# The last stage of a MoE-then-attention-convolution kernel, image by image in half-image slots

## The chip, the cores and the metric

One core of one Trainium2 chip runs the whole kernel. The metric is device microseconds of one launch. The kernel before takes 4912.13 us (median of 9 runs, 4890.7 to 4941.1). All data is 32-bit float in HBM at the start and at the end. The engines are TensorE (PE), VectorE (DVE), ScalarE (ACT), GpSimd (POOL) and SyncE (SP, used here to issue DMAs). Each has its own queue of instructions, works through it in order, and waits on semaphores of the others.

## What is computed

```python
# block 0: depthwise 7x7 conv, layer norm, mixture of 8 experts (2 per token), residual
x = depthwise_conv7x7(input) + dw_bias            # input: 32 x 128 x 56 x 56
x = layernorm_over_channels(x) * ln_gamma + ln_beta
moe = top2_of_8_experts_with_capacity(x)          # gelu MLP 128 -> 512 -> 128
h = input + x + layer_scale * moe
# block 1: coordinate attention, then a dense 3x3 convolution
y_h, y_w = h.mean(over w), h.mean(over h)         # pooled rows and columns
z = h_swish(bn1(w1 @ concat(y_h, y_w) + b1))      # 8 x (56 + 56)
a_h, a_w = sigmoid(wh @ z[:56] + bh), sigmoid(ww @ z[56:] + bw)
g = h * a_h * a_w                                 # the gated image
out = silu(bn2(conv3x3(g, wc) + bc))
...
```

## The kernel before

Four stages follow each other: the depthwise convolution (7x7, as matmuls with band matrices), the layer norm with the gates, the routing and the experts, and the last stage. The first three are the same in both kernels. They leave in HBM a table `acc_d` with one row of 137 numbers for each token in each of two parts: the row of a token's later expert (with the layer-normed x and that expert's share) and that of its earlier one. An image's sum is the two rows' first 128 numbers added.

The last stage works on pairs of images. There are 32 images, so 16 pairs; a pair has 6272 tokens, 49 tiles of 128.

- `load_pair` (L948) loads both images of x, 128 channels x 2 x 3136, in one DMA from SP.
- `combine` (L956 to L967), seven times a pair: two SP loads of 896 rows each (`cxn`, `cx2`; three buffers), POOL adds them (L959), PE transposes seven 128x128 tiles (L965), and DVE adds the transposed rows, beta and x into the image `x1` (L967). The first loads wait for a fence of DVE memsets (L855) behind the experts' last scatters.
- `squeeze` (L980 to L983): 1x1 matmuls of half an image into `pa`, then two DVE reductions (`rs`, `cs`).
- `attend`: the pooled sums (`rs` times weights L990, `ry` L991, PE L995 and L998), bn and h-swish on 8 partitions (`z`, L1001 to L1003), two matmuls (L1007, L1008), two sigmoids on ACT (L1009, L1010), then two gate products of 3136 elements on DVE (L1013 in place, L1014 into the padded image `pad`). Then POOL and ACT form, for the whole image at once, the six inputs `v` of a Winograd form F(4,3) along the rows: `t` (ACT L1021), `d` (POOL L1022), `twice` and `4d` (ACT L1024, L1025), `t` and the six sums (POOL L1026 to L1032).
- `conv` for half an image: six products k = 1, 2, 3, 4, 0, 5, three matmuls each (L1042; the profile counts each 32-bit matmul as two records), through five PSUM buffers. ACT copies product 1 (`odd`, L1047); DVE forms rows 0 and 1 of `y` from products 1 and 2 (L1048, L1049) and adds the other products in ten passes (L1052): four from product 3, four from 4, one each from 0 and 5. ACT applies silu (L1054) and issues the store (L1055).

The four halves' `conv` of a pair are spread over the seven `combine` steps of the next pair. The tile scheduler fixes each engine's order when the program is built, and adds the waits; inside an engine's queue nothing is overtaken at run time.

## Time and profile before

| what | value |
|---|---|
| median of 9 runs | 4912.13 us |
| profiled execution: run, span | 4901.19 us, 4899.2 us |
| busy in the span: PE, DVE, ACT, POOL | 3620.5 (74%), 2587.8 (53%), 1446.4 (30%), 2748.8 (56%) us |
| product matmuls L1042, 2304 records | 838.5 us |
| DVE passes L1052, 640 | 317.2 us, 552 ns each |
| POOL row adds L959, 112 | 269.6 us, 2415 ns each |
| POOL d L1022, 32 | 228.1 us, 7127 ns each |
| DVE gate products L1013, L1014, 32 each | 123.3 and 137.6 us |
| squeeze matmuls L980, 512 records | 146.0 us |
| transposes L965, 784 | 108.6 us |

Rows of a timeline give the start (us), the duration, engine, line and operation, output and inputs with their shapes, and in brackets the idle time before with what ended it. Matmuls overlap in the pipeline, so a row's duration is longer than the distance to the next start. A row with "x4" is a group of four that follow each other.

### The profile page before, as it was taken

To read this page: it belongs to the slowest core of one execution; us is meant where nothing else is said; L and a number is where in the kernel's file an instruction comes from. 1 tells how busy PE (TensorE), PEld (TensorE's weight loads), DVE (VectorE), ACT (ScalarE), POOL (GpSimd) and SP (SyncE) were. 2 spreads that over 40 slices of the span, in tenths; PEclk is the share of its full clock that TensorE was granted. 3 is DMA by queue.
4 is the path that set the end of the run, shared out by engine and by line. 5 is a ranking of instruction groups with operands and counts; after the bars stand their busy time and mean duration, and the time that the engine had idled before them with its cause. 6 is when DMAs were issued, how large, how long until landed. Compare 5 with 4: busy or idle time off the path is not lost. (4 is left out here: it accounts for less than half of the span.)

```text
span 4899.2 us, 60979 instructions
## 1 busy us (share of the span) xinstructions
PE 3620.5 (74%) x21765; PEld 2029.4 (41%) x21765; DVE 2587.8 (53%) x5562; ACT 1446.4 (30%) x3123; POOL 2748.8 (56%) x2044
## 2 busy tenths in 40 slices
PE   7999888841576486576457756677775999999999
PEld 4455588831233243233223323233332454444444
DVE  3333369996365267474411211111125888888887
ACT  0000066630233232233223323233341333332323
POOL 5444333421556654465555455555556978788875
PEclk9999997765688787788778877778887999999999
DMA  9999956549511211111111111111115555555552
GB/s 174 181 191 189 164 216 244 242 163 337 182 38 34 51 36 36 35 39 41 44 40 38 43 43 41 44 39 39 40 42 171 174 190 192 162 194 184 188 166 78
DMA packets 678004, 580.90 MB, mean 119 GB/s; under 512 B 405849, under 2 KB 611185, under 8 KB 667249
## 3 DMA queue, kind: packets, MB, share of 16 engines
q1 hardware_dynamic: 411408, 319.81, 22.7%
q10 hardware_dynamic: 222816, 160.70, 12.5%
q0 software_dynamic: 43264, 94.64, 7.2%
q8 instruction: 186, 3.05, 0.3%
q14 instruction: 330, 2.70, 0.2%
HBM read 314.92 MB, written 260.09 MB: 117 GB/s over the span
## 5 line engine op out<-in xcount | busy, mean ns | idle before, releaser
L703 POOL DMA_INDIRECT acc_d<-yo,row x676 | 700.6, 1036 | 760.3 <-issue 467.9
L662 PE MATMUL ph<-fxt,w 128*128 128x512 f32 (+1 forms) x1400 | 755.1, 677 | 378.2 <-ACT ht L663 346.7
L1042 PE MATMUL pc<-v,wk 128*128 128x392 f32 x1920 | 701.7, 508 | 0.4 <-POOL v L1027 0.4
L663 ACT ACTIVATE ht<-ph,bias 128x512 f32<-128x512 f32 (+1 forms) x700 | 473.4, 682 | 702.1 <-remote 306.6
L670 PE MATMUL py<-ht,w 128*128 128x512 f32 (+1 forms) x1400 | 653.7, 611 | 0.0
L641 POOL DMA_INDIRECT xg_r<-acc_d,idx x556 | 542.0, 975 | 198.7 <-issue 157.6
L165 PE MATMUL acc<-xs,band 28*64 28x432 f32 (+1 forms) x11264 | 535.6, 527 | 60.1 <-issue 37.8
L662 PEld LDWEIGHTS ph<-fxt,w 128*128 128x128 f32 x1400 | 279.1, 216 | 702.0 <-ACT ht L663 424.7
L1042 PEld LDWEIGHTS pc<-v,wk 128*128 128x128 f32 x1920 | 346.6, 190 | 306.8 <-issue 102.1
L165 PEld LDWEIGHTS acc<-xs,band 28*64 28x64 f32 x11264 | 299.0, 132 | 296.1 <-issue 199.0
L310 PE MATMUL lnps<-proj,lnyt 128*128 128x136 f32 x1568 | 364.8, 402 | 67.9 <-ACT sq L315 38.8
L670 PEld LDWEIGHTS py<-ht,w 128*128 128x128 f32 x1400 | 269.2, 201 | 284.9 <-issue 283.0
L310 PEld LDWEIGHTS lnps<-proj,lnyt 128*128 128x128 f32 x1568 | 351.0, 317 | 82.2 <-ACT sq L315 47.8
L654 DVE COPY fxt<-pt 128x512 f32<-128x512 f32 (+1 forms) x175 | 119.3, 682 | 445.7 <-remote 215.1
L697 DVE TENSOR_TENSOR ys<-pb,xg_r 128x512 f32<-128x512 f32 (+2 forms) x147 | 98.3, 671 | 450.0 <-PE pb L679 200.4
L1052 DVE SCALAR_TENSOR_TENSOR y<-pc,y 128x392 f32<-128x392 f32 x640 | 317.2, 552 | 11.7 <-PE pc L1042 11.7
L672 ACT ACTIVATE fyt<-py,b 128x512 f32<-128x512 f32 (+1 forms) x175 | 119.4, 682 | 674.9 <-PE py L670 472.2
L959 POOL TENSOR_TENSOR cxn<-cxn,cx 128x896 f32<-128x896 f32 x112 | 269.6, 2415 | 74.4 <-DMA cxn<-acc_d 25.8
L1022 POOL TENSOR_TENSOR d<-pad 128x3248 f32<-128x3248 f32 x32 | 228.1, 7127 | 143.6 <-DVE pad L1014 143.6
L448 PE MATMUL ps_r<-cnt_r,ones 128*128 128x1 f32 x400 | 84.1, 291 | 291.8 <-DVE junk L447 181.0
L181 DVE TENSOR_TENSOR yt<-acc,m 128x448 f32<-128x448 f32 x256 | 146.2, 619 | 264.4 <-PE acc L165 174.1
L641 POOL DMA_INDIRECT xg_f<-acc_d,idx x120 | 115.4, 962 | 224.4 <-DVE thr_r L460 90.0
(244 smaller groups left out, 5259.7 us busy)
## 6 DMA issues: line engine op xcount, KB each, us to landing
acc_d<-xn SPq DMA_DIRECT2D x16, 3356.5 KB
acc_d<-yo ACTq DMA_DIRECT2D x4, 13426.0 KB
lnyt<-y_d SPq DMA_DIRECT2D x16, 3136.0 KB
x<-in_x SPq DMA_DIRECT2D x16, 3136.0 KB
cxn<-acc_d SPq DMA_DIRECT2D x112, 448.0 KB
cx<-acc_d SPq DMA_DIRECT2D x112, 448.0 KB
out<-y ACTq DMA_DIRECT2D x64, 784.0 KB
xt<-in_x SPq DMA_DIRECT2D x64, 392.0 KB
```

Of the source, the lines that this page charges most:

```text
L165: nc.tensor.matmul(acc[r][half * M : (half + 1) * M, :, lo:hi], lhsT=band[rows, t0 + o - least, 1 - par : 1 - par + M], rhs=xs[i][rows, ha ...
L181: nc.vector.tensor_tensor(yts[r][:, :, i - 1 : W : 2], acc[r], common[r], ALU.add)
L310: nc.tensor.matmul(ps[:, j, :], lhsT=yf[:, self.j0 + g + j, :], rhs=proj, start=True, stop=True)
L641: d = nc.gpsimd.indirect_dma_start(out=xg[0:n, k, :], out_offset=None, in_=acc_d[0:T1, :], in_offset=bass.IndirectOffsetOnAxis(ap=idx[0][0 ...
L662: nc.tensor.matmul(ph[:, 0:N_], lhsT=w[0][:, f * P : (f + 1) * P], rhs=xt[:, 0:N_], start=True, stop=True)
L663: nc.scalar.activation(ht[:, f, 0:N_], ph[:, 0:N_], AF.Gelu, bias=w[2][:, f : f + 1])
L670: nc.tensor.matmul(py[:, 0:N_], lhsT=w2[:, f, :], rhs=ht[:, f, 0:N_], start=(f == 0), stop=(f == NF - 1))
L703: d = nc.gpsimd.indirect_dma_start(out=acc_d[:, :], out_offset=bass.IndirectOffsetOnAxis(ap=row[0:n, k : k + 1], axis=0), in_=yo[0:n, k, : ...
L959: nc.gpsimd.tensor_tensor(xn, xn, x2, ALU.add)
L1022: nc.gpsimd.tensor_tensor(d, high, low, ALU.subtract)
L1042: nc.tensor.matmul(m[k], lhsT=wk[k][:, dw, :], rhs=v[:, k, rows, dw : dw + W], start=(dw == 0), stop=(dw == 2))
L1052: nc.vector.scalar_tensor_tensor(r[x], m[k], f, r[y_], ALU.mult, ALU.add)
```

## The change

Only the last stage is rewritten. It goes image by image; image k has a slot, and the slot's list interleaves work on image k with products of image k-1 (upper half, `ch` 0) and k-2 (lower half, `ch` 1).

- x and the two parts of rows are loaded in blocks of eight image rows (448 tokens): one DMA of x and two of acc_d, 224 KB each, seven blocks an image, six buffers of each kind. The loads of block m+6 follow block m. Tables have 112 partitions x 4 tokens.
- The row adds of blocks with an even number (0, 2, 4, 6) run on POOL, of 1, 3, 5 on DVE. `merge` transposes four 112-token tiles and writes the eight rows at once into the padded image; the gate products then work in place there.
- `d`, `t` and `v` are formed for half an image at a time, in two parts; there is one buffer of `d` and of `t`, one `v` and one `y` for each half, and one `odd`.
- The small loads go to ACT's queue, the pads' borders alone are cleared (on DVE), and the stage's tiles wait for their own memory and not for the whole pool.

```diff
+    cp1 = ctx.enter_context(tc.tile_pool(name="cc", bufs=1, reuse_waits="tile"))
+    psp = ctx.enter_context(tc.tile_pool(name="cps", bufs=1, space=PSUM))
+    trp = ctx.enter_context(tc.tile_pool(name="ctr", bufs=2, space=PSUM))
+    pcp = ctx.enter_context(tc.tile_pool(name="cpc", bufs=5, space=PSUM))
+    MB = 8
+    NM = H // MB
+    MT = 2 * W
+    NX = 6
...
-            nc.sync.dma_start(t, a[name])
+        nc.scalar.dma_start(t, a[name])
...
+    def load_x(m):
+        nc.sync.dma_start(xss[m % NX], a["x"][m // NM][:, m % NM * MB : (m % NM + 1) * MB, :])
+    def load_rows(m):
+        for i, t in enumerate(cxs[m % NX]):
+            r0 = i * T1 + m * MB * W
+            d = nc.sync.dma_start(t, acc_d[r0 : r0 + MB * W, 0:C].rearrange("(j p) c -> p j c", p=MT))
+            for x in fence:
+                after(d.ins, x)
+    for m in range(NX):
+        load_x(m)
+    for m in range(NX):
+        load_rows(m)
...
-            nc.gpsimd.memset(t, 0.0)
+        nc.vector.memset(t[:, 0 : H + 2 : H + 1, :], 0.0)
+        nc.vector.memset(t[:, :, 0 : W + 2 : W + 1], 0.0)
...
+    def summed(m):
+        if m < NM * N:
+            x, x2 = cxs[m % NX]
+            (nc.vector if m % NM % 2 else nc.gpsimd).tensor_tensor(x, x, x2, ALU.add)
+    def merge(k, q):
+        m = NM * k + q
+        pt = trp.tile([P, BLK * P], F32, tag="tr", name=f"cpt{k}_{q}")[:, 0 : BLK * MT]
+        for j in range(BLK):
+            nc.tensor.transpose(pt[:, j * MT : (j + 1) * MT], cxs[m % NX][0][:, j, :], ident[0:MT, 0:MT])
+        nc.vector.scalar_tensor_tensor(pads[k % 2][:, 1 + q * MB : 1 + (q + 1) * MB, 1 : W + 1],
+                                       pt.rearrange("c (r w) -> c r w", w=W), beta_c, xss[m % NX], ALU.add, ALU.add)
+        if m + NX < NM * N:
+            load_x(m + NX)
+            load_rows(m + NX)
+        summed(m + 3)
...
+    def gate(n):
+        img = pads[n % 2][:, 1 : H + 1, 1 : W + 1]
+        nc.vector.tensor_tensor(img, img, bc(aw.unsqueeze(1), [C, H, W]), ALU.mult)
+        nc.vector.tensor_tensor(img, img, bc(ah.unsqueeze(2), [C, H, W]), ALU.mult)
+    def combined(n, ch, part):
+        v, pad = vs[ch], pads[n % 2]
+        r0 = 4 * RP * ch
+        byq = lambda x: x.rearrange("c (g r) w -> c g r w", r=4)
+        low, high = byq(pad[:, r0 : r0 + 4 * RP, :]), byq(pad[:, r0 + 2 : r0 + 2 + 4 * RP, :])
+        d, t = d_t, t_t
+        if part == 0:
             nc.scalar.mul(t, low[:, :, 1:3, :], 4.0)
             nc.gpsimd.tensor_tensor(d, high, low, ALU.subtract)
             nc.gpsimd.tensor_tensor(t, high[:, :, 1:3, :], t, ALU.subtract)
             nc.gpsimd.tensor_tensor(v[:, 1], t[:, :, 1, :], t[:, :, 0, :], ALU.add)
             nc.gpsimd.tensor_tensor(v[:, 2], t[:, :, 1, :], t[:, :, 0, :], ALU.subtract)
+        else:
+            nc.scalar.mul(v[:, 3], d[:, :, 1, :], 2.0)
+            nc.scalar.mul(d[:, :, 0:2, :], d[:, :, 0:2, :], 4.0)
+            nc.gpsimd.tensor_tensor(v[:, 4], d[:, :, 2, :], v[:, 3], ALU.subtract)
+            nc.gpsimd.tensor_tensor(v[:, 3], d[:, :, 2, :], v[:, 3], ALU.add)
             nc.gpsimd.tensor_tensor(v[:, 0], d[:, :, 2, :], d[:, :, 0, :], ALU.subtract)
             nc.gpsimd.tensor_tensor(v[:, 5], d[:, :, 3, :], d[:, :, 1, :], ALU.subtract)
...
+    def conv(n, ch, ks):
+        y = ys[ch]
+        r = [y[:, :, k, :] for k in range(4)]
+        m = {k: product(n, ch, k) for k in ks}
+        if 1 in m:
             nc.scalar.copy(odd, m[1])
             nc.vector.tensor_tensor(r[0], m[2], odd, ALU.add)
             nc.vector.tensor_tensor(r[1], odd, m[2], ALU.subtract)
...
+    def slots(k):
+        new = lambda f, *x: (lambda: f(*x)) if k < N else None
+        old = lambda d, f, *x: (lambda: f(k - d, *x)) if 0 <= k - d < N else None
+        cv = lambda *ks: old(2, conv, 1, ks)
+        pieces = [new(merge, k, 0), cv(1, 2), old(1, combined, 0, 1), new(merge, k, 1), new(merge, k, 2), cv(3),
+                  new(merge, k, 3), new(squeeze, k, 0), cv(4), new(merge, k, 4), new(merge, k, 5), cv(0), new(merge, k, 6),
+                  new(squeeze, k, 1), cv(5)]
+        cv = lambda *ks: old(1, conv, 0, ks)
+        pieces += [old(1, combined, 1, 0), new(pooled, k), cv(1, 2), new(attend, k), old(1, combined, 1, 1), cv(3),
+                   new(gate, k), cv(4), cv(0), cv(5), new(combined, k, 0, 0)]
+        return [f for f in pieces if f]
+    for m in range(3):
+        summed(m)
+    for k in range(N + 2):
+        for f in slots(k):
+            f()
```

In the new file the row add is L972, the transposes L978, the merge L979, the squeezes L990, their reductions L992 and L993, the weighting L998, `ry` L999, the pooled matmuls L1002 and L1005, `z` L1006 to L1008, the attention matmuls L1012 and L1013, the sigmoids L1014 and L1015, the gate products L1019 and L1020, `t` L1030 (ACT) and L1032 (POOL), `d` L1031, the v sums L1033 to L1041, `2d` and `4d` L1036 and L1037, the products L1049, `odd` L1058, rows 0 and 1 of y L1059 and L1060, the passes L1063, silu and store L1066 and L1067.

The scheduler again interleaves the lists by its own estimates. The order that the built program gives the engines in the slot of image k, once all stages of the pipeline are filled, is this ("(k,3)" is block 3 of image k, "product (k-1,0) 1" is product 1 of the upper half of image k-1, d0 and d1 are the d of upper and lower half):

```
POOL: row add (k,6) | d0 of k-1, t0, row add (k+1,0), v1, v2, v4, v3, row add (k+1,2), v0, v5 |
      t1, d1, v1, v2, v4, row add (k+1,4), v3, v0, v5 | row add (k+1,6)
ACT:  t0 of k-1, silu (k-2,0), 2d0, store, 4d0, t1, 2d1, 4d1, odd (k-1,0), silu (k-2,1), store,
      table load, two sigmoids of k, odd (k-1,1)
DVE:  merge (k,0), rows 0 1 of (k-2,1), merges (k,1) (k,2), 4 passes, merge (k,3), 1 pass, rs cs, 3 passes,
      merges (k,4) (k,5), row add (k+1,1), 1 pass, merge (k,6), 1 pass, row add (k+1,3), rs cs, weighting,
      row 0 of (k-1,0), ry, row 1, row add (k+1,5), z (with 2 passes between), 2 passes, 4 passes,
      gate product of k, 1 pass, gate product of k, 1 pass
PE:   products (k-2,1) 1 2 3 4 0 5 with merges' transposes and squeezes between,
      products (k-1,0) 1 2 and two of the three matmuls of 3, pooled matmuls (wait for ry),
      the rest of 3, product 4, attention matmuls (wait for z), products 0 5
```

In the slot of image 1, where nothing of k-2 exists, POOL's order is d0, t0, v4, v1, v2, v3, v0, v5, two row adds, d1; ACT has 2d1, odd (0,0) and 4d1 ahead of the two sigmoids of image 1; `ry` stands ahead of row 0 on DVE.

On SP, the second table load of block (k+1,5) waits for POOL's row add (k,6), and what follows it in the queue waits with it.

More of the change, by code (lines that the diff above doesn't have):

```diff
@@ new lines, in moe_conv_then_coordatt_kernel @@
+    xss = [cp1.tile([C, MB, W], F32, name=f"xs{k}") for k in range(NX)]
+    cxs = [[cp1.tile([MT, BLK, C], F32, name=f"cx{i}_{k}") for i in range(2)] for k in range(NX)]
+    def load_x(m):
[6 more added lines that the diff above has]
+                after(d.ins, x)
@@ new lines, in moe_conv_then_coordatt_kernel @@
+    for k in range(1, 5):
+        nc.vector.tensor_scalar(wk[k], wk[k], 1.0 / 6.0 if k > 2 else -1.0 / 6.0, None, ALU.mult)
+    nc.vector.tensor_scalar(wk[0], w0, 0.25, None, ALU.mult)
+    w1t = cp1.tile([C, QP], F32, name="w1t")
+    nc.vector.memset(w1t, 0.0)
+    nc.scalar.dma_start(w1t[:, 0:MIP], a["w1"])
+    quarter = [x / 56 for x in (7.0, 3.0, 1.0, 1.0)]
+    wq = cp1.tile([P, 4], F32, name="wq")
+    for k in range(4):
+        nc.vector.memset(wq[:, k : k + 1], quarter[k])
+    pick = [ident[:, QP * j : QP * j + MIP] for j in range(4)]
@@ new lines, in squeeze @@
+    def squeeze(n, half):
+        pad = pads[n % 2]
+        for j in range(4):
+            r0 = 1 + (4 * half + j) * SR
+            nc.tensor.matmul(pa[j * QP : (j + 1) * QP, 0 : SR * W], lhsT=w1t, rhs=pad[:, r0 : r0 + SR, 1 : W + 1],
+                             start=True, stop=True)
+        nc.vector.tensor_reduce(rs[:, half], pa[:, 0 : SR * W].rearrange("p (r q v) -> p r q v", r=SR, q=4), AX.X, ALU.add)
+        nc.vector.tensor_reduce(cs[:, half, :], pa[:, 0 : SR * W].rearrange("p (r w) -> p w r", r=SR), AX.X, ALU.add)
```

274 lines of the change are left out of this document (90 added, 184 removed).

## The prediction

> **What bounds the kernel now.** I read the page's slices first, then the stretches of the last stage, then its chain of waits, then the timeline of one pair of images, engine by engine. All times are of the one profiled execution (span 4899.2 us, run 4901.19 us; the median of the runs is 4912.13 us, 11 us more). The last stage, the only one that the change touches, begins when TensorE (PE) stops at 3699.8 us and lasts to the end: 1199 us. Two of its stretches:
>
> ```profile
> 3700.00:3720.00 20.00, 0.00 (x0) 0.00 (x0) 11.24 (x43) 0.00 (x0) 12.29 (x16) 0.57 0.36 122
> ...
> 4100.00:4250.00 150.00, 142.01 (x547) 74.81 (x546) 129.24 (x174) 45.59 (x45) 114.24 (x48) 1.00 0.58 185
> ```
>
> The numbers are busy us of PE, weight loads, VectorE (DVE), ScalarE (ACT), GpSimd (POOL), then the granted clock and the DMA share. In steady state PE is busy 95%, DVE 86%, POOL 76%; at the start PE has nothing. The chain of waits gives the beat, the same place in two successive pairs:
>
> ```profile
> 4064.11 6.12 PE pc L1042 x18
> ...
> 4134.62 6.12 PE pc L1042 x18
> ```
>
> 70.5 us for two images, 35.25 us each. PE's timeline holds where it waits:
>
> ```profile
> 4127.14 2.24 PE L1042 MATMUL pc<-v,wk 128*128 128x392 f32 x6
> 4130.41 0.36 PE L995 MATMUL cpa<-ry,ident 128*8 128x14 f32 x8 [1.03 <-DVE ry L991]
> ...
> 4133.97 0.42 PE L1007 MATMUL cpa<-z,wht 8*128 8x56 f32 x2 [0.82 <-DVE z L1003]
> ```
>
> Two waits for DVE, about 2.1 us an image. So an image is 33.15 us of PE work and 2.1 us of waiting: PE bounds the steady state. DVE's and POOL's timelines show what stretches DVE:
>
> ```profile
> 4100.41 3.41 DVE L1013 TENSOR_TENSOR x<-x,aw 128x3136 f32<-128x3136 f32 x1
> 4103.74 0.55 DVE L1052 SCALAR_TENSOR_TENSOR y<-pc,y 128x392 f32<-128x392 f32 x1
> ...
> 4128.20 1.91 DVE L990 TENSOR_TENSOR rs<-rs,wq 128x56 f32<-128x56 f32 x1
> ```
> ```profile
> 4109.19 7.16 POOL L1022 TENSOR_TENSOR d<-pad 128x3248 f32<-128x3248 f32 x1 [3.43 <-DVE pad L1014]
> 4116.26 3.11 POOL L1026 TENSOR_TENSOR t<-pad,t 128x1624 f32<-128x1624 f32 x1
> 4119.29 2.11 POOL L959 TENSOR_TENSOR cxn<-cxn,cx 128x896 f32<-128x896 f32 x1
> 4121.34 1.64 POOL L1027 TENSOR_TENSOR v<-t 128x812 f32<-128x812 f32 x1
> ...
> 4127.97 2.07 POOL L959 TENSOR_TENSOR cxn<-cxn,cx 128x896 f32<-128x896 f32 x1
> ```
>
> The 56-element L990 took 0.35 us at 3742.23, where POOL was idle; here it ends at 4130.11, just after POOL's row add (4130.04). A DVE instruction with both inputs in SBUF waits out the POOL instruction that runs. The reverse holds: at 3770.40 a v sum of POOL took 4.94 us instead of 1.76, behind a gate product of DVE. ACT's timeline, for the copy that starts a product's DVE passes:
>
> ```profile
> 4116.39 0.88 ACT L1024 ACTIVATE twice<-d 128x812 f32<-128x812 f32 x1 [2.29 <-POOL d L1022]
> 4117.30 1.56 ACT L1025 ACTIVATE d<-d 128x1624 f32<-128x1624 f32 x1
> ...
> 4126.47 0.48 ACT L1047 COPY odd<-pc 128x392 f32<-128x392 f32 x1 [2.40 <-PE pc L1042]
> ```
>
> Now ACT does d's multiples soon after d, one block for the whole image, and then idles until the product.
>
> **The change, part by part.**
>
> **PE work: no change.** Same 36 product matmuls (0.66 us each, from 18 records in 5.93 us) and eight squeezes an image; 28 transposes of 112 columns for 24.5 of 128: the same 3136 columns. Ten product runs instead of eight add two switches of 0.19 us (2 records take 0.85, their share of a long run 0.66); the squeezes pair up a little better. 33.2 us an image.
>
> **DVE: +1.8 us of work.** Three row adds an image (96 of 224): 512 elements at the gate product's 3.41/3136 = 1.09 ns are 0.6 us, each with a wait behind POOL. POOL's instructions are halved, so a wait is 0 to 1.2 us where the unhalved ones cost 1.0 to 2.0.
>
> **POOL: about 2.4 us less work** (four row adds of 1.2 us, 2.05 x 512/896, for 3.5 of 2.05; the rest halved and doubled in number). Nothing from that alone: POOL was not the bound.
>
> **Half images and the order.** Here I expect the loss. In the built program ACT's queue holds, in every slot: 2d and 4d of the second half, then the copy "odd" of product (k-1,0), then the rest. So the copy waits for the second d on POOL, which stands behind the whole first half. DVE's r0 (L1059) waits for the copy, and the reduction ry stands behind r0 in DVE's queue; PE's pooled matmuls (L1002) wait for ry, z follows, then the sigmoids and the two gate products, and the next image's first d waits for these. That is a closed loop over four engines, once per image. From the end of one second gate product to the next:
>
> - POOL: row add 1.2, d 3.55, t 1.5, add 1.2, v1 and v2 1.6, v4 and v3 1.75, add 1.2, v0 and v5 1.9, t 1.5, d 3.55 = 18.95 us (halves of the start-to-start times 7.1, 3.0, 1.6, 1.75, 1.9). Halving isn't exact: 812 elements start 1.59 us apart, 1624 need 3.01, which leaves 0.17 fixed, so ten halves cost 0.85 more: 19.8.
> - POOL held up by DVE's adds: two of 0.6 fall here, 0 to 1.2; I take 0.6.
> - ACT: 0.45 + 0.8 + 0.5 = 1.75 (halves of 0.88 and 1.56, the copy).
> - DVE: r0 0.5, ry 0.2; then r1 0.5, row add 0.6 with a wait of 0 to 1.2 (I take 1.0, a row add of POOL being next to it), z 0.35, a pass 0.5, r 0.2, a pass 0.5, z 0.15 with a wait of 0 to 1.2 (0.6: mean of the ends), six passes 2.85, gate 3.4, pass 0.45, gate 3.4 = 15.2. The sigmoids (1.2 us from L1012) hide under the six passes.
> - six hand-overs of 0.05: 0.3.
>
> Sum 19.8 + 0.6 + 1.75 + 15.2 + 0.3 = 37.65; I take **37.6 us** a slot. Bounds: all uncertain waits at nothing and POOL's first row add done before the gate (it needs rows asked for only after the transposes of (k,0), some 5 us before the gate ends) give 33.4, below PE's own 33.2 + 1.8 = 35.0, so 35; all at their tops 39.1, and late row loads 40. PE then idles 4.4 us a slot.
>
> On such idling the trace says: after 5.08 us of waiting (3847.20) the clock was 0.50 and twelve product records took 6.53 us instead of 4.22; after 2.53 us (3885.64) it stayed whole. [...] By the rows a drop costs 2.3 us of PE, which has 4.4 to spare: the sum stays too.
>
> **Loads.** 21 DMAs of 224 KB an image on SP's one queue instead of 7.5 larger ones. SP's issue takes 0.36 us: 7.6 of 37 us. Bytes are the same, DMA share stays near 0.56. Rows arrive at 346 GB/s (3726 to 3730 us), so one load moves in 0.7 us; the tightest has 6 us (rows (k+1,5), asked for after the transposes of (k,6), read by DVE's third add). Cost nothing; the cover gone, it is rival 3.
> [...]
>
> **Start.** Rows can leave at 3709.7, when the fence's memsets end, instead of 3714.35 behind fifteen small loads, and no longer share with a 3.1 MB image (7 us at 445 GB/s). DVE's constants, 3709.7 to 3721.6 before, lose POOL's pad memset beside them (3.6 us) and waits on loads: to 3717. Then three adds, seven merges, four reductions and their turns with PE, 10 us; z and sigmoids 6; gates with adds between 8: image 0 gated at 3741 (before 3755.4). Image 1: POOL's first-slot order 17.0, ACT 2.4, gates 7.25: 3768 (before 3786.4). Gain 18 us, uncertain by 8.
>
> **End.** After the last gate product: 2 products (4.1) and three halves at 11.86 us (4872.84 to 4884.70) less the 9.4 us run since the sigmoid matmul, 30.3, and the tail after the last product pass begins, 6.7: 37 to 38 (before 51.6, four halves). Gain 13.6.
>
> Sum: 3768 + 30 x 37.6 + 38 = 4934, against 4899.2: +35 us. Before: 3786.4 + 30 x 35.37 + 51.6. The two ends give 32 us back, 30 slots lose 67. Even at 36.4 us a slot.
>
> **Rivals.**
> 1. *PE still bounds (faster).* If POOL reaches the second d 2.6 us earlier (row add before the gate, adds that don't meet), the loop falls to 35: 3768 + 1050 + 38 = 4856, -43 us. For it: POOL has only 26 us of work; against: the loop's order is fixed in the queues and PE has no part in it. It decides from 36.4 us a slot downwards.
> 2. *Even.* Slots of 35.9 to 36.9 us: the ends' gains pay for the loop. Time within 15 us.
> 3. *Loads late.* SP's queue is in order, and a load behind a wait on POOL's last add holds up the others; if rows take over 6 us, DVE's third add stalls in the loop: 39.5 us, 4991, +92. Against: DMA share 0.58, and waits on row loads were 18 us in 840.
>
> **How the numbers follow.** Forecast (37 to 39 us a slot) 0.55, rival 1 0.22, rival 2 0.15, rival 3 0.08. On the median: 4912 + 35 = 4947, said as 4946. The likeliest case alone spans 4929 to 4989; with rival 1 the range is 4872 to 4990. Faster by over 0.3% (15 us, about what a measurement here tells from no change) 0.22, same 0.15, slower 0.63.
>
> **What would show it.** A beat of 37 to 38 us between gate products; PE's longest wait, 2 to 4 us, before L1002 for ry; before it r0 waiting for "odd", the copy for 4d, that for POOL's second d; POOL's d waiting for the gate. Wrong if L1002's wait is under 1 us, if the beat is 35, or if row adds wait on DMA.

## The result, and the profile after

The changed kernel takes 5071.95 us, median of 14 runs (5061.28 to 5088.6). The kernel before takes 4911.97 us, median of 46 (4882.72 to 4941.1). The ratio is 1.0329, with an interval of 1.0313 to 1.0346: slower by 160 us, where 35 were forecast. The direction was right; the time lies above the range. The profiled execution has a span of 5059.2 us.

The stretches come first (window, its length, busy us of PE, weight loads, VectorE (DVE), ScalarE (ACT) and GpSimd (POOL), granted clock, DMA share, GB/s):

```profile
3700.00:3720.00 20.00, 2.27 (x9) 1.51 (x10) 9.45 (x56) 0.00 (x0) 7.74 (x11) 0.55 0.51 131
4150.00:4300.00 150.00, 123.81 (x470) 64.45 (x468) 135.92 (x156) 42.40 (x49) 106.83 (x73) 0.92 0.56 157
```

PE was busy 95% of its steady state and is now busy 83%. DVE is the busiest engine, 91%, though it was given little work; the DMA share is about what it was (0.56 for 0.58).

The last stage begins when PE ends its last expert matmul, here at 3699.2 us. It took 1199.4 us before and takes 1360.0: this is the whole loss. Three pieces make it up. The time from its start to the second image's second gate product was 86.7 us and is 82.8. The mean beat between gate products was 35.37 us and is 41.24. The time from the last gate product to the end was 51.6 us and is 40.0. Both ends gained, 15.5 us together; thirty slots lost 5.87 us each.

The chain of waits of one slot (start, us, what; between the same place in two successive slots):

```profile
4059.56 4.15 PE pc L1049 x12
...
4080.13 1.18 DVE pad L979 x2
4081.31 1.28 DVE cx L972
4082.60 7.70 issue
4090.30 0.55 DVE y L1063
4090.85 0.60 DVE pad L979
4091.45 0.04 issue
4091.50 1.52 PE pa L990 x4
...
4100.55 4.15 PE pc L1049 x12
```

41.0 us for a slot. Up to 4078 the chain is PE's own work; then it goes through DVE: two merges, one of the new row adds (L972), 7.70 us in which the chain names no releaser, the merge of block 6, and only then the second half's squeeze. DVE's timeline shows what the 7.70 us are, and POOL's what went on meanwhile:

```profile
4080.05 1.26 DVE L979 SCALAR_TENSOR_TENSOR pad<-cpt,beta_c,xs 128x448 f32<-128x448 f32 x2
4081.23 9.14 DVE L972 TENSOR_TENSOR cx<-cx,cx 112x512 f32<-112x512 f32 x1
...
4091.84 2.06 DVE L972 TENSOR_TENSOR cx<-cx,cx 112x512 f32<-112x512 f32 x1
...
4096.49 0.68 DVE L972 TENSOR_TENSOR cx<-cx,cx 112x512 f32<-112x512 f32 x1
```
```profile
4080.89 1.06 POOL L1040 TENSOR_TENSOR v<-d_t 128x406 f32<-128x406 f32 x1
4081.89 1.07 POOL L1041 TENSOR_TENSOR v<-d_t 128x406 f32<-128x406 f32 x1
4082.91 1.64 POOL L1032 TENSOR_TENSOR t_t<-pad,t_t 128x812 f32<-128x812 f32 x1
4084.49 3.62 POOL L1031 TENSOR_TENSOR d_t<-pad 128x1624 f32<-128x1624 f32 x1
4088.05 0.91 POOL L1033 TENSOR_TENSOR v<-t_t 128x406 f32<-128x406 f32 x1
4088.91 0.92 POOL L1034 TENSOR_TENSOR v<-t_t 128x406 f32<-128x406 f32 x1
4089.78 1.42 POOL L1038 TENSOR_TENSOR v<-d_t,v 128x406 f32<-128x406 f32 x1
```

The same add takes 0.68 us when it meets nothing (4096.49). The one at 4081.23 found L1040 running, and POOL then started L1041, L1032, L1031, L1033 and L1034 ahead of it. It got in at about 4089.7 (its end less 0.68 us), where L1038 is the longer for it (1.42 us; the same sum took 0.97 at 4077.63). So it did not wait only for the instruction that was running; it lost five changes from one POOL instruction to the next. A "lost change" is counted so from here on: a POOL instruction that started while a DVE instruction with inputs in SBUF was held up. I counted them from the records of the last stage: of the 96 adds on DVE 38 lost none, 6 one, 26 two, 1 three, 17 five and 8 six.

The page's groups of the row adds (count, busy us and mean ns, then idle time before them):

```profile
L972 POOL TENSOR_TENSOR cx<-cx,cx 112x512 f32<-112x512 f32 x128 | 204.6, 1599 | 401.1 <-DMA cx<-acc_d 203.1
...
L972 DVE TENSOR_TENSOR cx<-cx,cx 112x512 f32<-112x512 f32 x96 | 378.5, 3943 | 4.4 <-DMA cx<-acc_d 4.3
```

3.94 us against 0.68: 3.26 us of being held up on the mean, three times an image. Most of it falls on the first of the three, which stands ahead of block 6's merge: its records are 7.9 us long on the mean (9.0 to 10.3 in nearly all late slots), the second's 2.8 and the third's 1.1. PE pays at the squeeze behind it, as its longest waits say (us in total, times, longest; over 1000 us from 3900):

```profile
PE pa L990 <- DVE pad L979: 165.0, 24, 7.8
```

6.9 us an image. Behind such a wait PE is slow as well: from 4091.5 to 4093.0 the granted clock is 0.50, as it is over the first 1.5 us behind each of the 26 waits of 5.0 to 7.9 us from 3925 on. Its timeline has groups of the same sizes at a clock of 1.00 before (4078 to 4083) and after it (4097 to 4100):

```profile
4082.45 0.85 PE L990 MATMUL pa<-pad,w1t 128*32 128x392 f32 x4
...
4091.50 1.52 PE L990 MATMUL pa<-pad,w1t 128*32 128x392 f32 x4 [6.68 <-DVE pad L979]
4092.95 3.70 PE L1049 MATMUL pc<-v,wk 128*128 128x392 f32 x8
...
4097.07 2.90 PE L1049 MATMUL pc<-v,wk 128*128 128x392 f32 x8
```

1.5 us more in this slot. The wait and the slow work are about the 8.0 us between 41.24 and PE's own 33.2.

### The profile page after: what moved, and what is told of

Its sections match the earlier page's. It is cut to its first block, busy times and chain, and to the rows that moved or that the text cites. A ratio compares the mean times of both kernels' runs of the same rounds, so it can differ in the third digit from the quotient of the medians.

```text
span 5059.2 us, 62785 instructions
## 1 busy us (share of the span) xinstructions
PE 3685.3 (73%) x21877; PEld 2035.1 (40%) x21877; DVE 2815.9 (56%) x5668; ACT 1463.0 (29%) x3219; POOL 2733.6 (54%) x2309
## 5 line engine op out<-in xcount | busy, mean ns | idle before, releaser
L1049 PE MATMUL pc<-v,wk 128*128 128x392 f32 x2304 | 871.7, 521 | 0.0
L165 PE MATMUL acc<-xs,band 28*64 28x432 f32 (+2 forms) x11264 | 555.8, 541 | 54.8 <-DVE yt L181 25.5
L1049 PEld LDWEIGHTS pc<-v,wk 128*128 128x128 f32 x2304 | 432.2, 199 | 357.4 <-issue 129.9
L972 POOL TENSOR_TENSOR cx<-cx,cx 112x512 f32<-112x512 f32 x128 | 204.6, 1599 | 401.1 <-DMA cx<-acc_d 203.1
L165 PEld LDWEIGHTS acc<-xs,band 28*64 28x64 f32 x11264 | 286.7, 136 | 323.4 <-issue 228.5
L972 DVE TENSOR_TENSOR cx<-cx,cx 112x512 f32<-112x512 f32 x96 | 378.5, 3943 | 4.4 <-DMA cx<-acc_d 4.3
L1063 DVE SCALAR_TENSOR_TENSOR y<-pc,y 128x392 f32<-128x392 f32 x640 | 327.3, 551 | 27.1 <-PE pc L1049 26.1
L990 PE MATMUL pa<-pad,w1t 128*32 128x392 f32 x512 | 160.5, 589 | 189.4 <-DVE pad L979 189.4
```

The lines of the kernel that those rows point to most:

```text
L165: nc.tensor.matmul(acc[r][half * M : (half + 1) * M, :, lo:hi], lhsT=band[rows, t0 + o - least, 1 - par : 1 - par + M], rhs=xs[i][rows, ha ...
L972: (nc.vector if m % NM % 2 else nc.gpsimd).tensor_tensor(x, x, x2, ALU.add)
L990: nc.tensor.matmul(pa[j * QP : (j + 1) * QP, 0 : SR * W], lhsT=w1t, rhs=pad[:, r0 : r0 + SR, 1 : W + 1], start=True, stop=True)
L1049: nc.tensor.matmul(m, lhsT=wk[k][:, dw, :], rhs=vs[ch][:, k, :, dw : dw + W], start=(dw == 0), stop=(dw == 2))
L1063: nc.vector.scalar_tensor_tensor(r[x], m[k], f, r[y_], ALU.mult, ALU.add)
```

## The experiments

The theories were these. The forecast's ring of four engines is right and only its term for the adds' waits is too small; then adds that aren't held up give about 37.6 us a slot (theory A in the expectations). Or the adds as work are too much for either engine; then the place they go to decides. Or the ring is tied by ACT's order ("odd" behind 4d); then moving that copy decides (G). Or PE bounds once DVE is free. Later came one on the shape: that a tile of 112 partitions is what makes DVE lose (D), against one by which POOL keeps DVE out whenever its own next instruction is ready (E). How a shape would do that, no run shows; "the port" in the expectations is the author's name for whatever lets one of the two engines in at a time, and no run shows it either.

A diff is against the changed kernel unless another is named. The table has the ratio to the kernel before on the same chip, and three numbers of the one profiled execution: the last stage, the mean beat, and from the stage's start to the second image's second gate product. Some chips ran the stages ahead of the last one some 580 us faster (in e1 it began at 3122.7 us, in the kernel before at 3699.8), so different runs are compared by the stage, one execution each. The ratio says how a run lies to the kernel before on its own chip; on a faster chip the same microseconds make a larger ratio (e1's 1.0361 is 151 us, the changed kernel's 1.0329 is 160).

| run | ratio (95%) | stage, us | beat, us | start, us |
|---|---|---|---|---|
| before | 1 | 1199.4 | 35.37 | 86.7 |
| after | 1.0329 (1.0313 to 1.0346) | 1360.0 | 41.24 | 82.8 |
| e1 all adds on POOL | 1.0361 (1.0311 to 1.0411) | 1346.8 | 40.27 | 99.9 |
| e2 no adds | 0.9877 (0.9845 to 0.991) | 1155.8 | 34.58 | 78.7 |
| e3 all adds on DVE | 1.0432 (1.0396 to 1.0468) | 1391.0 | 42.02 | 90.6 |
| e4 odd adds on PE | 1.0152 (1.0117 to 1.0187) | 1275.4 | 38.24 | 89.3 |
| e5 adds over 128 partitions | 1.0143 (1.0111 to 1.0176) | 1259.9 | 37.73 | 87.8 |
| e6 the same, all on POOL | 1.0283 (1.0248 to 1.0317) | 1352.8 | 40.79 | 89.0 |
| e7 odd adds at the merge | 1.0105 (1.0056 to 1.0154) | 1275.2 | 38.39 | 83.6 |
| e8 as e5, adds over 112 | 1.0187 (1.015 to 1.0225) | 1297.9 | 38.86 | 92.0 |
| e9 as e5, weighting on PE | 1.0463 (1.0433 to 1.0493) | 1429.9 | 43.51 | 85.6 |
| e10 as e9, adds on POOL | 1.04 (1.0357 to 1.0444) | 1382.6 | 41.8 | 89.5 |
| e11 adds by DMA | 1.0053 (1.0032 to 1.0073) | 1231.9 | 35.87 | 116.1 |
| e12 as e11, "odd" ahead of 2d | 1.0038 (1.0019 to 1.0057) | 1221.0 | 35.58 | 114.2 |
| e13 as e12, first image as before | 0.9985 (0.9964 to 1.0007) | 1198.5 | 35.75 | 86.6 |
| e14 as e13, DVE's small products off SBUF | 0.9906 (0.9879 to 0.9933) | 1158.8 | 34.47 | 85.7 |
| e15 as e14, "odd" ahead of 2d | 0.9894 (0.987 to 0.9917) | 1157.0 | 34.37 | 87.5 |

### Where the adds run: e1, e2, e3

```diff
-            (nc.vector if m % NM % 2 else nc.gpsimd).tensor_tensor(x, x, x2, ALU.add)
+            nc.gpsimd.tensor_tensor(x, x, x2, ALU.add)
```

> All seven row adds of an image on POOL, none on DVE; nothing else is edited. Theory A (the port): the loss beyond the predicted 37.6 us a slot is that DVE's row adds (three an image, 13 us of recorded time for 2 us of work) are shut out by POOL's instructions as long as these follow each other without a pause. Then DVE's stalls go, POOL gets 3 x 1.25 = 3.8 us more, and the beat between second gate products falls from 41.2 to 37 to 40 us: 4940 to 5020 us. Theory B (the ring of the prediction alone sets the beat, and the adds' long records only fill time that DVE would wait for the copy 'odd' anyway): POOL's part of the ring grows by up to 3.8 us, beat 42 to 45, 5100 to 5190 us. Theory C (the adds wait for row loads): POOL waits for the same loads, beat 41, about 5070.

In e2 the line is left out, and in e3 it is `nc.vector.tensor_tensor(x, x, x2, ALU.add)`.

> The row adds are left out: only the first of the two table rows of each token goes into the image; the loads of both stay. A: DVE's 13 us and POOL's 5 us of adds go, the ring falls to about 32 us, and PE sets the beat at 35 to 36 us: 4850 to 4900 us. B: the ring loses POOL's adds (3.6 us) and no more, beat 37.5, about 4950 us. C: the loads are as they were, beat 41, about 5060 us.

> All seven row adds on DVE, none on POOL. A: seven adds an image can be shut out instead of three, while POOL's own chain is 5 us shorter; beat 41 to 47 us, 5070 to 5250 us, with single adds of 5 to 10 us. B: the ring loses POOL's adds, beat 37 to 38.5 us, 4940 to 4980 us. C: beat 41, about 5070 us.

Without the adds (e2) the slot falls to 34.58 us on the mean, and PE bounds the late ones (the stretches' columns):

```profile
3500.00:4100.00 600.00, 596.95 (x2366) 314.57 (x2367) 470.94 (x756) 211.72 (x251) 387.91 (x286) 1.00 0.49 151
```

The mean has two parts. Nothing reads the second table in e2, so its loads ran ahead: 241 row loads from 3200 to 3500 us, at a DMA share of 1.16 to 1.18, against 63 from 3600 to 3900. Loads lie on the chain of the early slots, which take 35 to 39 us; the late ones take 32.9 and 33.6, with lighter loads (share 0.49) than the changed kernel has. The changed kernel's chain has no load from 3860 to 4980, so the difference in loads is not what separates the two there. So the half images, the merges and the order of products cost PE nothing by themselves: the 6.7 us a slot between the means, 8.5 between the late slots (41.7 and 33.2), come with the adds. Taking them off DVE (e1) does not bring it back. There the weighting of `rs`, 56 elements, is held up instead, in DVE's and POOL's timelines:

```profile
3642.49 15.26 DVE L998 TENSOR_TENSOR rs<-rs,wq 128x56 f32<-128x56 f32 x1
```
```profile
3642.04 3.61 POOL L1031 TENSOR_TENSOR d_t<-pad 128x1624 f32<-128x1624 f32 x1
3645.60 1.63 POOL L1032 TENSOR_TENSOR t_t<-pad,t_t 128x812 f32<-128x812 f32 x1
...
3656.41 1.26 POOL L972 TENSOR_TENSOR cx<-cx,cx 112x512 f32<-112x512 f32 x1
```

Eleven POOL instructions, from L1032 at 3645.60 to the add at 3656.41, started while it was held up: 15.26 us for an instruction of 0.2 us. The loss is therefore not the adds' own; another DVE instruction with inputs in SBUF, beside a run of POOL instructions, has it in their place.

In e3, with no adds on POOL, DVE's adds lost no change, and yet the beat was the longest so far:

```profile
L972 DVE TENSOR_TENSOR cx<-cx,cx 112x512 f32<-112x512 f32 x164 | 199.2, 1215 | 0.0
```

Seven adds of 1.2 us an image lie on DVE there, and POOL waited 18.5 us a slot for the gate products. The queues' orders differ as well. PE's longest wait there is for POOL's first sum behind the gate (`v` L1033, 4.8 us a slot), so another ring, from the gate products over POOL to the next products, seems to set its 42 us; no run tests that. So held-up adds are not the only way to a slot of 41 us.

### Odd adds without SBUF's second input: e4, e7

e4 leaves the odd blocks' second tables to PE, which adds them up in PSUM, and transposes the others by the same matmul.

```diff
...
-            nc.tensor.transpose(pt[:, j * MT : (j + 1) * MT], cxs[m % NX][0][:, j, :], ident[0:MT, 0:MT])
+            ts = cxs[m % NX] if q % 2 else cxs[m % NX][:1]
+            for i, t in enumerate(ts):
+                nc.tensor.matmul(pt[:, j * MT : (j + 1) * MT], lhsT=t[:, j, :], rhs=ident[0:MT, 0:MT], start=(i == 0), stop=(i == len(ts) - 1))
```

> DVE's three adds an image go to PE: for odd blocks both tables are transposed into the same PSUM tile, the second matmul accumulating on the first; POOL keeps its four adds. PE gets 3 x 0.55 = 1.65 us an image, DVE has no add at all. A: PE has 34.9 us of work and sets the beat with some waiting, 36 to 37 us, 4875 to 4930 us. B: ring less DVE's add, 36.6, or 40 if the adds were only filler, 4900 to 5030 us. C: beat 41, about 5070 us.

The beat is 38.24 us and PE is never idle (899.28 us of 900). The matmuls cost more than the transposes that they replace; PE's timeline of e4:

```profile
3864.80 1.04 PE L981 MATMUL cpt<-ident,cx 112*128 112x112 f32 x8
```

One table's four tiles are eight records and 1.04 us, where its four transposes took 0.55 (at 4081.97 in the changed kernel). Ten tables at 1.04 us in place of seven at 0.55 are some 6 us of PE an image by the records; the beat is 5.0 us over PE's 33.2. With DVE free, PE is the next bound.

e7 transposes both tables of an odd block and adds the second at the merge, from PSUM:

```diff
...
+            if i == 0:
+                nc.vector.scalar_tensor_tensor(rows, pt, beta_c, xss[m % NX], ALU.add, ALU.add)
+            else:
+                nc.vector.tensor_tensor(rows, pt, rows, ALU.add)
...
```

> The changed kernel with DVE's three adds an image left out: for odd blocks PE transposes both tables, and DVE merges twice from PSUM (PSUM and SBUF as inputs, which waited for POOL nowhere so far). PE +1.65 us, DVE 3 x 0.67 for 3 x 0.6 and the waits; POOL keeps its four adds over 112 partitions. Theory A (DVE's SBUF adds are the loss): beat 35 to 37 us, stage 1170 to 1235 us, 30 us under to 35 us over the kernel before. Theory B (ring): 37 to 38.5 us, 1230 to 1280 us. If the small DVE instructions with SBUF inputs are shut out in place of the adds: 38 to 40 us, 1265 to 1330 us.

38.39 us. The wait at the adds is gone, and others stand in its place: DVE's weighting of `rs` takes 1.13 us instead of 0.2, `z` 0.88, `r_t` 0.71, and POOL's adds 2.04. On DVE these make some 2 us a slot; the rest of it was not followed up.

### The shape and the order: e5, e6, e8

e5 makes the tables' tiles 128 partitions high, loads 112 of them and adds over all; e6 does the same with every add on POOL; e8 is e5 with the adds over `t[0:MT]` again.

```diff
-    cxs = [[cp1.tile([MT, BLK, C], F32, name=f"cx{i}_{k}") for i in range(2)] for k in range(NX)]
+    cxs = [[cp1.tile([P, BLK, C], F32, name=f"cx{i}_{k}") for i in range(2)] for k in range(NX)]
+    for p in cxs:
+        for t in p:
+            nc.vector.memset(t[96:P], 0.0)
...
```

> The changed kernel with the row adds of both engines over all 128 partitions instead of 112 (rows 112 to 127 of the tables' tiles are zeros, set once at the start: up to 5 us). In the changed kernel a DVE add lost up to seven changes from one POOL instruction to the next, and in the kernel with all adds on DVE it lost none of 140; what is missing there is POOL's 112-partition adds between its 128-partition sums. [...] Then here no DVE instruction waits for more than the one POOL instruction that runs, the adds take 0.7 to 4 us, beat 37 to 38.5 us, the last stage 1225 to 1285 us (changed kernel 1360), 25 to 85 us over the kernel before. Theory E (POOL keeps the port whenever its next instruction is ready): as the changed kernel, adds of 9 us, beat 41, stage 1350 to 1370, 150 us over.

> All seven adds on POOL and over 128 partitions (run e1_pool_adds with the tables' tiles filled up). D: the weighting of the squeezed sums on DVE, held up to 15 us there, waits for one POOL instruction at most; beat 35 to 37.5 us, stage 1170 to 1250 us, between 30 us under and 50 us over the kernel before. E: as e1_pool_adds, beats of 35 to 49 us, mean 40, stage about 1347, 150 us over.

> Run e5_add128 (tiles of 128 partitions, same order of instructions on every engine) with the adds back on 112 partitions, for both engines. Theory D (the 112-partition adds are what lets POOL keep the port): adds of up to 9 us on DVE again, several changes of POOL's instruction lost, beat 40 to 41.5 us, stage 1330 to 1370 us. Rival E2 (the order of POOL's queue was what helped in e5_add128): as there, no change lost, beat 37.7, stage 1250 to 1270 us.

In e5 none of DVE's 96 adds loses a change, but for one that began together with a POOL instruction; they take 1.31 us on the mean, and the beat is 37.73 us, where the forecast's sum had 37.6. DVE's and POOL's timelines of e5 show the ordinary case, each waiting for one instruction of the other:

```profile
4321.94 2.44 DVE L1001 TENSOR_TENSOR rs<-rs,wq 128x56 f32<-128x56 f32 x1
4324.30 2.13 DVE L975 TENSOR_TENSOR cx<-cx,cx 128x512 f32<-128x512 f32 x1
```
```profile
4320.69 3.61 POOL L1034 TENSOR_TENSOR d_t<-pad 128x1624 f32<-128x1624 f32 x1
4324.26 1.62 POOL L1035 TENSOR_TENSOR t_t<-pad,t_t 128x812 f32<-128x812 f32 x1
4325.84 1.41 POOL L1041 TENSOR_TENSOR v<-d_t,v 128x406 f32<-128x406 f32 x1
```

The weighting gets in as L1034 ends, and the add as L1035 ends. But 128 partitions also changed the order that the scheduler chose, so e5 alone doesn't tell the shape from the order. e8 has e5's orders and the old shape: 94 of its 96 adds lose nothing either. Most of the way from 1360.0 to 1259.9 us thus goes with the order (to 1297.9); what differs there is POOL's queue (the places of its adds, and of L1038 in the second half) and DVE's (the second add of an image stands behind the weighting instead of ahead of the second squeeze). The rest, 38 us of stage, goes with the shape, and there it is the weighting that differs, in the same surroundings; e8's timelines:

```profile
4126.63 3.41 DVE L1001 TENSOR_TENSOR rs<-rs,wq 128x56 f32<-128x56 f32 x1
```
```profile
4124.72 3.64 POOL L1034 TENSOR_TENSOR d_t<-pad 128x1624 f32<-128x1624 f32 x1
4128.30 1.63 POOL L1035 TENSOR_TENSOR t_t<-pad,t_t 128x812 f32<-128x812 f32 x1
```

Here it sits through L1035 as well. In e8 29 of 32 weightings lose a change or more (median 3.40 us), in e5 none (1.99 us). That favours theory D, but e6 goes against it as the whole cause: with 128 partitions throughout, 7 of its 32 weightings lost two to eleven changes, up to 15.27 us, and the beat is 40.79. The intervals of e5 and e8 overlap a little (1.0111 to 1.0176, and 1.015 to 1.0225), so the shape's share of the whole time rests on the records rather than on the medians.

### Weighting on PE: e9, e10

e9 is e5 with the weighted sum over each row's quarters done by PE; e10 has the adds on POOL too, and eight buffers instead of six.

```diff
...
-        nc.vector.tensor_tensor(rs, rs, bc(wq.unsqueeze(1).unsqueeze(1), [P, 2, SR, 4]), ALU.mult)
-        nc.vector.tensor_reduce(ry, rs, AX.X, ALU.add)
-            nc.tensor.matmul(py[:, 0:H].rearrange("m (k j r) -> m k j r", k=2, j=4)[:, :, j, :], lhsT=pick[j], rhs=ry,
-                             start=True, stop=True)
+            for v in range(4):
+                nc.tensor.matmul(py[:, 0:H].rearrange("m (k j r) -> m k j r", k=2, j=4)[:, :, j, :],
+                                 lhsT=pick_q[min(v, 2)][:, QP * j : QP * j + MIP], rhs=rs[:, :, :, v], start=(v == 0), stop=(v == 3))
```

> Run e5_add128 without the two DVE instructions between the squeeze and PE's pooled matmuls (the weighting rs x wq and the sum ry): PE weights and sums instead, with 16 tiny matmuls for 4, from selection matrices scaled once at the start. In e5_add128 the weighting waited 2.4 us for POOL's second d and the add behind it 2.1 us for t, both in front of ry. Theory F (the ring closes over DVE's two-input instructions that wait for POOL between squeeze and z): z comes earlier by 2 to 4 us, beat 34.5 to 36.7 us, stage 1160 to 1225 us. Theory G (the ring of the prediction: the copy 'odd' behind ACT's 4d behind POOL's second d, r0 ahead of ry): z no longer stands behind r0, but the passes and gates do; beat 37 to 38, stage 1240 to 1265 us.

> As e9_pick, with all seven adds on POOL (128 partitions) and eight buffers for the loads instead of six: three of the adds stand behind the second half's sums, where POOL waited for the gates. Theory F: DVE has no instruction with two SBUF inputs between squeeze and gate but z's last; POOL's 30 us fit into PE's 34: beat 34.5 to 36 us, stage 1160 to 1205 us, from 40 us under the kernel before to level with it. Theory G: POOL's part of the ring grows by up to 3.8 us, beat 38 to 41, stage 1270 to 1350 us.

Both missed. In e9 the scheduler put DVE's adds ahead of `z`, and the adds wait for their rows; its longest waits over 1000 us:

```profile
POOL cx L974 <- DMA cx<-acc_d: 215.6, 13, 19.1
...
DVE cx L974 <- DMA cx<-acc_d: 84.8, 16, 10.0
```

This is the forecast's rival 3, which the changed kernel shows in its first slots only: three pieces of its chain from 3799 to 3840 are such loads (5.41, 5.12 and 6.10 us), and none from 3860 to 4980. In e10 the held-up instruction is `r_t`, 8x112 elements with one input in SBUF:

```profile
4342.85 6.87 DVE L1008 TENSOR_SCALAR r_t<-z_t 8x112 f32<-8x112 f32 x1
```

4.18 us on the mean, and 17 of 32 lost two to eleven changes. So an instruction with a single input in SBUF was held up here as those with two were, and by as many POOL instructions as the weighting of e1, eleven.

### Adds by DMA: e11 to e15

e11 has one tile a block; the second table's rows are added to it by a DMA that accumulates, issued by POOL five blocks ahead, with ten buffers.

```diff
...
-            (nc.vector if m % NM % 2 else nc.gpsimd).tensor_tensor(x, x, x2, ALU.add)
+            r0 = T1 + m * MB * W
+            d = nc.gpsimd.dma_start(cxs[m % NX], acc_d[r0 : r0 + MB * W, 0:C].rearrange("(j p) c -> p j c", p=MT),
+                                    accum_op=ALU.add)
...
```

> No engine adds rows: the second table's rows are added by DMA into the first's tile (seven accumulating DMAs of 224 KB an image issued from POOL's queue, about 1 us of POOL each by its rows of 0.96 us for an indirect DMA; ten single buffers, five blocks ahead). DVE has no add, POOL 7 us of issues for 5 us of adds, most of them behind the second half's first sums. Theory A (the adds' waits are the loss, the halves are not): ring 19.8 - 3.6 + 1 for POOL's part, 34 us, so PE sets the beat, 33.5 to 35.5 us, stage 1130 to 1195 us, from 70 us under the kernel before to level with it. Rival H (accumulating DMAs hold up POOL, waiting for the first rows in its queue, or land late): beat 37 to 42, stage 1240 to 1390 us. Theory G (the copy 'odd' behind ACT's 4d behind POOL's second d closes the ring): PE's longest wait is 1 to 4 us before the pooled or the attention matmuls, beat 35 to 37.

e12 adds to it a dependency that puts ACT's 2d of the second half behind the copy "odd":

```diff
...
+            if ch == 1 and 0 in last_odd:
+                tc.add_manual_dep(twice.ins, last_odd[0].name, mybir.DependencyInfo(mybir.DependencyClass.NoSync, mybir.DependencyReason.DATA),
+                                  reason="the copy first")
...
```

> Run e11_acc10 with the copy 'odd' of product (k-1,0) put ahead of the second half's 2d and 4d in ACT's queue (DVE's order is the same; POOL's second-half sums v3, v4, v0, v5 move behind the next accumulating DMAs). Theory G: r0 no longer waits for POOL's second d; if the ring set e11's beat it falls by 1 to 3 us; if PE set it, no change beyond 0.5 us, or a rise where the late sums hold up the gates or the next products (up to 3 us). Theory A without G: no gain.

35.87 and 35.58 us: 5.4 and 5.7 us a slot less than the changed kernel, but a start over 30 us later, since the accumulating loads came after all the first loads. The dependency is worth 0.3 us between two single executions; the ratios' intervals overlap. e13 is e12 with the first image's tables loaded apart and added as before, and eight buffers:

```diff
...
+        if m < NM:
+            (nc.vector if m % 2 else nc.gpsimd).tensor_tensor(cxs[m], cxs[m], cx2[m], ALU.add)
+        elif m < NM * N:
...
```

> Run e12_acc10_odd with eight buffers and the first image's rows added by POOL and DVE from plain loads, loads of rows ahead of later x blocks: in e11 and e12 the first gate came 30 us later than in the changed kernel, since the accumulating DMAs started only after all first loads. Start as in the changed kernel (second gate 80 to 95 us after the stage begins instead of 114), beat as e12, 35.0 to 36.0 us: stage 1175 to 1210 us, between 25 us under and 10 us over the kernel before.

The start is back (86.6 us). What is left over PE's beat lies on DVE's small instructions: the weighting takes 1.88 us and `r_t` 0.91 on the mean of 700 us in e13, where 0.2 would do. The mean hides that slots alternate from the third on: where the weighting takes 3.3 to 3.6 us, the slot takes 38.3 to 39.5; where it takes 0.2 to 0.9, the slot takes 32.9 to 33.2, in one and the same execution. e14 takes them out of POOL's way: the weighting to PE as in e9, `z` kept in PSUM, and no dependency for "odd"; e15 is e14 with the dependency.

```diff
...
-        nc.vector.tensor_scalar(z_t, py, s1, o1, ALU.mult, ALU.add)
-        nc.vector.tensor_scalar(r_t, z_t, 3.0, 0.0, ALU.add, ALU.max)
-        nc.vector.scalar_tensor_tensor(z_t, r_t, 6.0, z_t, ALU.min, ALU.mult)
+        nc.vector.tensor_scalar(py, py, s1, o1, ALU.mult, ALU.add)
+        nc.vector.tensor_scalar(r_t, py, 3.0, 0.0, ALU.add, ALU.max)
+        nc.vector.scalar_tensor_tensor(z_t, r_t, 6.0, py, ALU.min, ALU.mult)
```

> As e13 with ACT's queue as in e11 (the copy 'odd' behind 2d and 4d), and no DVE instruction with two SBUF inputs between squeeze and gates: PE weights and sums the squeezed sums (as in e9_pick), z stays in PSUM. In e11 the weighting took 2.4 us (0.2 alone) and z's last step 0.8 (0.25 alone). Theory F (these waits for POOL close what is left of the ring): beat 33.3 to 34.7 us, stage 1125 to 1170. Theory G (the copy 'odd' behind POOL's second d): DVE's z stands behind r0, r0 behind the copy; beat stays 35.5 to 37, stage 1190 to 1235, with PE waiting for z.

> As e14 with the copy 'odd' ahead of the second half's 2d and 4d (as in e12). F: as e14, 33.3 to 34.7 us. G: 1 to 3 us less than e14. Both: beat 33.3 to 34.5, stage 1125 to 1165 us, 35 to 75 us under the kernel before.

The group of `r_t` in e15 (count, busy us and mean ns, idle time before), then the same stretch of e13 and of e15:

```profile
L1013 DVE TENSOR_SCALAR r_t<-pa 8x112 f32<-8x112 f32 x20 | 5.2, 261 | 0.7
```
```profile
4000.00:4700.00 700.00, 669.66 (x2575) 350.60 (x2574) 559.86 (x819) 228.13 (x275) 690.65 (x450) 0.97 0.82 179
```
```profile
4000.00:4700.00 700.00, 700.00 (x3174) 369.80 (x3173) 525.19 (x818) 239.97 (x286) 698.43 (x470) 1.00 0.86 187
```

PE goes from 96% to 100%, its clock from 0.97 to 1.00, and the beat from 35.75 to 34.37 us, though PE was given twelve more small matmuls an image. No weighting is left to be held up, `r_t` takes 0.26 us, and `z`'s last step 0.25. e15 is faster than both kernels: 4830.83 us against 4879.43 on its chip, ratio 0.9894 (0.987 to 0.9917), and by the two ratios 4.2% faster than the changed one. Its stage is 42.4 us shorter than before's: 30 slots of 1.00 us and 13.3 us at the end, less 0.8 at the start. The dependency for "odd" gives 0.1 us a slot, again with intervals that overlap.

## Why the prediction was right or wrong

The forecast's sum was 4934 us for the span; it was 5059.2. The 125 us lie in three terms: the start 14 (the second image's second gate ended at 3782.0 us, not 3768), the thirty slots 30 x (41.24 - 37.6) = 109, and the end 2 (40.0 for 38).

**The step that failed** is the one for DVE's row adds: "POOL's instructions are halved, so a wait is 0 to 1.2 us where the unhalved ones cost 1.0 to 2.0". It priced being held up as the rest of one POOL instruction. The changed kernel's adds were held up 3.26 us on the mean, and up to 9.6, because DVE lost up to six changes. The forecast also has no term for the add that did the harm: its ring enters DVE at r0, while the first add of an image stands ahead of block 6's merge and the second squeeze. Halving POOL's instructions doesn't help, since the wait isn't bounded by one of them. A hint was in the trace of before: a weighting of 0.35 us that sat through more than the one instruction that it met.

```profile
4092.59 2.04 DVE L990 TENSOR_TENSOR rs<-rs,wq 128x56 f32<-128x56 f32 x1
```

It began as POOL changed from L1030 (which ended at 4092.68) to L1031, and ended with L1031, at 4094.63; 11 of the 32 in that trace met such a change within 0.05 us of their start and lost it.

**The ring** was there, closed by another link. In 24 late slots of the changed kernel the records give the same three parts: 1.1 us from the end of the second gate product to POOL's d, 20.4 us (18.6 to 21.4) from there until POOL lets the first add in, and 20.2 us from there to the end of the next second gate product, 41.7 in all. In 23 of the 24 the add got in as POOL came to L1038 of the second half, whether its record was 9.0 or 10.3 us long. So the length of its record matters less than its place: the merge and the squeeze behind it wait for POOL's run over both halves. The forecast had 20.4 us for POOL's part (19.8 + 0.6) and 17.25 for ACT, DVE and the hand-overs. In e5 the weighting takes the add's place in it, let in as POOL's second d ends: 1.1, 19.2 and 17.5 us in the same slots, and a beat of 37.73 for 37.6. The length thus came right there, but in part by luck, since the forecast has no wait of the weighting.

**The link that closes it** was put on "odd" waiting behind 4d on ACT. In the changed kernel's chain from 3860 to 4980 us no instruction of ACT stands; the delay is ahead of the second squeeze, on DVE (7.70 of 41.0 us), and PE's longest wait stands before L990. Before L1002, where it was to show, no wait was over 0.8 us from 3900 to 4900. Freeing "odd" gave 0.3 us (e12) and 0.1 us (e15), in kernels whose adds are done by DMA; in the changed kernel itself it was not tried.

**The clock** was given no cost ("the sum stays too"). But the slow squeeze and products stand behind the held-up add, in the ring's last part, and took 1.5 us more in the slot shown above. The reading behind it was wrong too: after the 2.53 us of waiting at 3885.64 in the trace of before the clock did not stay whole. It was 0.50 from 3887.2 to 3890.4, and twelve product records took 5.91 us instead of 4.22:

```profile
3886.22 5.91 PE L1042 MATMUL pc<-v,wk 128*128 128x392 f32 x12
```

So there a drop followed a wait of 2.53 us, as one followed the wait of 5.08 us at 3847.20.

**The start** lost 14 of the 18 us forecast as a gain. Image 0 was gated at 3746.4 us (forecast 3741), image 1 35.6 us later (forecast 27). Two held-up adds lie in it (6.33 us at 3746.93, 3.64 us at 3761.68), but the chain there doesn't go through them: it has 8.31 us of a row load up to 3743.6, POOL's row add behind it, and POOL's first sums. From 3723 to 3735 the DMA moved 248 to 250 GB/s at a share of 1.17 to 1.19, where the forecast took 346. What the held-up adds cost at the start is not shown. **The end** came within 2 us of the forecast. **PE's work** came as forecast too: without adds (e2) the late slots take 32.9 and 33.6 us, for 33.2. **Loads** were no bound once the slots were full: the chain has none from 3860 to 4980 us, though POOL's row adds waited for rows for 203 us in the whole stage.

One bound is summed wrongly: with the four terms that it names taken off, the loop's 37.65 us become 34.25, not 33.4; and the 1.8 us of waiting in PE's 35.0 is not derived (the trace of before had 2.1). Nothing else rests on either.

**Rival 1** (PE bounds, 35 us a slot, 4856 us) needed POOL to reach the second d earlier. PE did bound where nothing in the ring was held up: in e2's late slots, with the adds left out (33.2 us), and in e14 and e15, with the adds given to the DMA and the small DVE instructions read from PSUM or given to PE (34.5 and 34.4 us). **Rival 2** fell with the beat. **Rival 3** gave the nearest time (4991) for another reason; its mechanism appears in e9 and in the first slots. The range's top, 4990, came from the same bound of 1.2 us for a wait, so it could not hold a cause of which it had the mechanism and not the size.

**What stays open** is what lets DVE in at a change. Orders with like neighbours gave 0 and 11 lost changes; the height of 112 partitions matters at one order (e8 and e5) and 128 doesn't cure it at another (e6, e10). That a weighting beside a long run of POOL loses more often is only what the counts suggest. The beats of e3 and e7 weren't traced to their end either.

## What to carry to other kernels

In these runs an instruction of DVE with its inputs in SBUF was held up not by one GpSimd instruction but by up to eleven in a row (e1): price it by the whole run in GpSimd's queue beside it, and look in the trace for a small instruction that took several times its shortest time. Ask what stands behind it in its queue, and whether GpSimd's run begins with something that this work releases: that is a ring without any semaphore at one of its links, and the profile's chain shows that link as "issue" (7.70 us in the slot above). Where such an instruction lies on a ring over the engines, moving it from one engine to the other did not help here (e1, e3: beats of 40.27 and 42.02 us); taking its inputs out of SBUF or its work off DVE did, by reading from PSUM, by a matmul, or by letting a DMA add (e14, e15: 34.47 and 34.37 us). Cost such a wait by the longest one that the trace shows, beside the mean.

## What the runs showed of the hardware

How long one instruction can be held up: 0.2 us of work took 15.26 us while POOL started eleven instructions (e1), and eight partitions with a single SBUF input took 6.87 us (e10). With its input in PSUM the same instruction, `r_t`, took 0.26 us on the mean of twenty in e15, where POOL was busy 698.43 of 700 us. The accumulating DMA takes POOL 0.76 us an issue in e15's steady stretch (141 issues, from the start of one to the start of POOL's next instruction, 0.71 to 1.02), less than the 1.23 us of the add that it replaces (from 4074.68 to 4075.91 in the changed kernel). The records of the issues are longer, 2.39 us on the mean, but overlap those of the instructions behind.
